# Channel sums of the norms moved from matmuls to adds, and the feed-forward's way back on four column groups

## The chip, the cores and the metric

The kernel runs on one core of a Trainium2 chip. The metric is the device time of one execution in microseconds, the median of several runs. The engines are named as in the profile: PE (TensorE, matmuls), PEld (its weight loads), DVE (VectorE), ACT (ScalarE), POOL (GpSimd) and SP (SyncE, which here only issues DMAs). Each engine runs its own instructions strictly in the order of the program.

## What is computed

Eight images x[384, 32, 32] go through two layers. Layer 0: an RMS norm over the 384 channels, a Mamba block (input projection, causal convolution, softplus deltas, a state scan with 16 states, gates, output projection) run in both directions over the 1024 positions, a depthwise 3x3 convolution with a sigmoid, and the residual. Layer 1: layer norm over the channels, causal attention with 6 heads of 64, residual; layer norm, a feed-forward of 384 to 1536 to 384 whose two weights are Kronecker products, residual.

```python
def rmsnorm(x, w, eps=1e-06):
    return x * jax.lax.rsqrt(jnp.mean(x * x, axis=-1, keepdims=True) + eps) * w

def step(h, inp):
    dA, dBu, c = inp
    h = dA * h + dBu
    return (h, jnp.einsum('bdn,bn->bd', h, c))

t = t + attn(_ln_t(t), ...)
w_fc, w_proj = jnp.kron(c_fc_1, c_fc_2), jnp.kron(c_proj_1, c_proj_2)
t = t + gelu(_ln_t(t) @ w_fc.T) @ w_proj.T
```

## The kernel before

**Layout.** Channels lie on the 128 partitions, so a tensor of one image is three channel tiles (c = 0, 1, 2) of 128 x 1024; positions are split in two halves of 512[...]. A batch is one image. Everything is float32 but the spread of the scan's input, which is bfloat16 in three parts.

**The stages of a batch b**, each a function: `project` (RMS norm, input projection), `gates`, `prepare` (causal convolution), `deltas` (softplus and what feeds the scan), `scans` (96 groups of 128 lanes each), `local` (3x3 convolution), `finish` (output projection, residual), `layernorm`, `attention`, `mix` (output projection, residual), `forward`. One scan group is: a DMA that broadcasts delta into a dA tile (one of 12 buffers), exp on ACT (L994), two small matmuls that spread the input (L1004, tile b), and for each half a multiply (L1009) and a scan (L1017) on DVE, then a product with C on POOL (L1020) and a sum by matmuls on PE (tile y, four column groups at a time). After each two block directions come uz on DVE (L970) and POOL (L975).

**Sums over channels.** They go across partitions and over three tiles, and are done on PE with a 128 x 128 matrix of ones, which leaves the sum on every partition. Each takes three matmuls that accumulate in one bank (`accumulate`, L422): in `project` over the squares (tile pss, L690), in `center` over the values (pm_a of the attention's norm, pm_f of the feed-forward's, L1068), in `deviation` over the squares of the centred values (pv_a, pv_f, L1091). `center` then subtracts on DVE (L1075), `deviation` squares on ACT (L1087, tiles lsq) and takes the reciprocal root on ACT (`rsqrt_mean`, L335 and L336), and `layernorm` multiplies on DVE (L1108).

**Feed-forward.** The Kronecker factor reduces the 384 inputs to 32 rows (tile y there named fy), PE makes 1536 hidden rows from them in pairs of banks (ph, `wide`), ACT applies gelu into a tile g that holds two of them (L1369), and `back` (L1373) accumulates them into bank pz, 32 output rows per matmul. A pair of hidden tiles goes to two of the four column groups of the array, and two such pairs make one round a; there are three rounds in each half.

**The order of the work** is not written out by hand. All stages record their operations in a `Plan` with an engine, a cost and a due time (`at`), and `Plan.run` (L170) places them greedily: of the operations ready on an engine the one due first is next. Four PSUM banks of kind psm, three of kind b, one y, 26 SBUF tiles of kind t and the 12 dA tiles are given out in that order as well. The due times come from windows (`PROJECT`, `NORM`, `FORWARD` and so on, L436 to L444), given in periods from the start of a batch's scans, from `PERIOD` and `HEAD` (L1401), and from offsets such as `EVICT`, `LOAD` and `PARTS`; `STAY` favours ACT operations that need no other function table, and `BACKLOG` limits how far SP issues DMAs ahead. The result is a fixed program: in the steady part of it, `project` and `gates` of batch b+2, `prepare` and `deltas` of b+1 (or so), and `finish` to `forward` of earlier batches stand among the scans of batch b.

Of the kernel before, what the change touches and what calls it, by code (L numbers as in the profile page):

```python
# [17 lines left out]
P = 128  # L18
B, C, H, W = 8, 384, 32, 32
L = H * W  # L20
CT = C // P
# [70 lines left out]
def pe(n, k=1):  # L92
    return k * (0.02 + n * 0.00185)
# [11 lines left out]
class Plan:  # L105
# [1 line left out]
    DRAIN = 0.19  # L107
    SLACK = 0.1
    SWITCH = 1.3
    STAY = 15.0  # L110
    BACKLOG = 10.0
    LANDING = 1.0
    DMA_LATENCY, DMA_RATE = 2.5, 262e3

# [173 lines left out]
def conv_attn_hybrid_kernel(  # L288
# [41 lines left out]
    def mm(out_, lhsT, rhs, first=True, last=True):  # L330
        return nc.tensor.matmul(out_, lhsT=lhsT, rhs=rhs, start=first, stop=last)  # L331
# [6 lines left out]
    def half(hf):  # L338
        return slice(hf * HALF, (hf + 1) * HALF)
# [93 lines left out]

    EVICT, MOVE, SUMS, PRODUCTS, DECAY, LOAD, PARTS = 27.83, 13.24, 12.22, -9.17, -222.27, -783.55, -339.2  # L436

    PROJECT, GATES, CONV, DELTA = (-1.525, -1.398), (-1.067, -0.985), (-0.952, -0.894), (-0.917, -0.358)
    LOCAL, OUTPUT, NORM, ATTEND = (0.593, 0.969), (1.016, 1.081), (1.16, 1.227), (1.191, 1.755)
    MIX, FORWARD = (1.81, 1.845), (1.879, 2.092)  # L440

    PROJECT0, EARLY, CONV0, DELTA0 = (-373.152, -337.008), (-788.581, -96.07), (-84.26, 78.46), (50.858, 257.144)
    GATES0, ZEROS, LATE, PROJECT1, GATES1 = (253.962, 443.889), (24.114, 455.177), (161.216, 306.444), (-92.709, 246.406), (452.944, 585.724)
    CONV1, DELTA1, LAYER1 = (164.85, 479.335), (392.72, 578.245), (462.639, 791.646)  # L444

    class Window:

# [216 lines left out]
    def project(b):  # L664

        xt = []
        for c in range(CT):
            t = tl(f"xt_{b}_{c}")
            dma(lambda t=t: t.t, lambda c=c: x[b, chans(c)].rearrange("p h w -> p (h w)"), [], [t], P * L * 4)
            xt.append(t)  # L670
        win = in_weights(b, 0)
        xp = [tl(f"xp_{b}_{c}", [P, PADDED]) for c in range(CT)]
        for c in range(CT):

            def border(c=c):
                xg = xp[c].t.rearrange("p (h w) -> p h w", w=WP)
                nc.gpsimd.memset(xg[:, 0 : H + 2 : H + 1, :], 0.0)
                nc.gpsimd.memset(xg[:, 1 : H + 1, 0 : W + 2 : W + 1], 0.0)

            op("POOL", 0.3, border, [], [(xp[c], "border")])  # L680
        sq = []
        for c in range(CT):
            t = tl(f"sq_{b}_{c}")
            op("ACT", act(L), lambda t=t, c=c: nc.scalar.activation(t.t, xt[c].t, AF.Square), [xt[c]], [t])
            sq.append(t)
        for hf in range(NH):
            p = bank(f"pss_{b}_{hf}")

            accumulate(
                [(lambda p=p, hf=hf, c=c: (p.t, ones, sq[c].t[:, half(hf)]), [sq[c]]) for c in range(CT)], p, pe(HALF), xp  # L690
            )
            op("ACT", 2 * act(HALF) + 0.1, lambda p=p: rsqrt_mean(p.t, eps6), [], [p], table=EXP)
            for c in range(CT):

                def scaled(p=p, hf=hf, c=c):
                    nc.vector.scalar_tensor_tensor(
                        inside(xp[c].t, hf), grid(xt[c].t[:, half(hf)]), col("norm_w", c), grid(p.t),
                        ALU.mult, ALU.mult,
                    )

                op("DVE", dve(HALF), scaled, [xt[c], p], [(xp[c], hf)])
        project.of[b] = xp
        into(b, 0, xp, win)
# [356 lines left out]

    def center(dst, src, n):

        for hf in range(NH):
            p = bank(f"pm_{n}_{hf}")

            accumulate(  # L1068
                [(lambda p=p, hf=hf, c=c: (p.t, ones, src[c].t[:, half(hf)]), [(src[c], hf)]) for c in range(CT)],
                p, pe(HALF), dst,  # L1070
            )
            for c in range(CT):
                op(
                    "DVE", dve(HALF),
                    lambda p=p, hf=hf, c=c: nc.vector.scalar_tensor_tensor(  # L1075
                        dst[c].t[:, half(hf)], p.t, -1.0 / C, src[c].t[:, half(hf)], ALU.mult, ALU.add
                    ), [p, (src[c], hf)], [(dst[c], hf)],
                )

    def deviation(dst, n, hf):  # L1080

        sqs = [tl(f"lsq_{n}_{hf}_{i}") for i in range(2)]
        p = bank(f"pv_{n}_{hf}")
        for c in range(CT):
            op(
                "ACT", act(HALF),
                lambda c=c: nc.scalar.activation(  # L1087
                    sqs[c // 2].t[:, half(c % 2)], dst[c].t[:, half(hf)], AF.Square
                ), [(dst[c], hf)], [(sqs[c // 2], c % 2)], holds=sqs,
            )  # L1090
        accumulate(  # L1091
            [
                (lambda c=c: (p.t, ones, sqs[c // 2].t[:, half(c % 2)]), [(sqs[c // 2], c % 2)])
                for c in range(CT)
            ], p, pe(HALF),
        )
        op("ACT", 2 * act(HALF) + 0.1, lambda: rsqrt_mean(p.t, eps5), [], [p], table=EXP)
        return p

# [228 lines left out]
    def forward(b, x2):  # L1328

        xn2 = [tl(f"xn2_{b}_{m}") for m in range(CT)]  # L1330
        center(xn2, x2, f"f{b}")
        y, z = tl(f"fy_{b}"), tl(f"fz_{b}")
        for hf in range(NH):
            p = bank(f"py_{b}_{hf}")

            accumulate(
                [
                    (
                        lambda p=p, hf=hf, c=c: (p.t, kr1[:, c].rearrange("p r i -> p (r i)"), xn2[c].t[:, half(hf)]),
                        [(xn2[c], hf)],  # L1340
                    )
                    for c in range(CT)
                ], p, pe(HALF), [y],
            )
            op("ACT", act(HALF), lambda p=p, hf=hf: nc.scalar.copy(y.t[:, half(hf)], p.t), [p], [(y, hf)])

            q = deviation(xn2, f"f{b}", hf)
            op(
                "DVE", dve(HALF), lambda q=q, hf=hf: nc.vector.tensor_mul(y.t[:, half(hf)], q.t, y.t[:, half(hf)]),
                [q], [(y, hf)],  # L1350
            )
        for hf in range(NH):
            pz = bank(f"pz_{b}_{hf}")
            for a in range(FT // RG):
                for r0 in range(0, RG, 2):

                    ph = [bank(f"ph_{b}_{hf}_{a}_{r0 + i}") for i in range(2)]

                    def wide(ph=ph, a=a, r0=r0, hf=hf):
                        for i in range(2):  # L1360
                            rows = slice((r0 + i) * KI, (r0 + i + 1) * KI)
                            mm(ph[i].t, w_fc1.t[rows, a, :], y.t[rows, half(hf)])

                    g = tl(f"g_{b}_{hf}_{a}_{r0}")
                    op("PE", pair(HALF), wide, [(y, hf), w_fc1], ph, holds=[g])

                    def gelu(ph=ph, g=g):
                        for i in range(2):
                            nc.scalar.activation(g.t[:, half(i)], ph[i].t, AF.Gelu)  # L1369

                    op("ACT", 2 * act(HALF), gelu, ph, [g], table=GELU)

                    def back(pz=pz, g=g, a=a, r0=r0):  # L1373
                        for i in range(2):
                            r = r0 + i
                            mm(
                                pz.t[r * KI : (r + 1) * KI, :], w_p1.t[:, a * RG + r, :], g.t[:, half(i)], a == 0,
                                a == FT // RG - 1,
                            )

                    op("PE", pair(HALF), back, [g, w_p1], [pz], holds=[z])
            op("ACT", act(HALF), lambda pz=pz, hf=hf: nc.scalar.copy(z.t[:, half(hf)], pz.t), [pz], [(z, hf)])
        ob = out[b].rearrange("(c p) h w -> c p (h w)", p=P)
        for m in range(CT):
            for hf in range(NH):
                p = bank(f"pe_{b}_{m}_{hf}")
                op(
                    "PE", pe(HALF), lambda p=p, m=m, hf=hf: mm(p.t, kr2.t[:, chans(m)], z.t[:, half(hf)]),
                    [(z, hf), kr2], [p],
                )  # L1390

                def add(p=p, m=m, hf=hf):
                    t = x2[m].t[:, half(hf)]
                    nc.vector.tensor_add(t, p.t, t)

                op("DVE", dve(HALF), add, [p], [(x2[m], hf)])
            dma(lambda m=m: ob[m], lambda m=m: x2[m].t, [x2[m]], [], P * L * 4)

    PERIOD, HEAD = 418.62, 167.66  # L1401

    def stretch(span, b):
        return Window(span[0] * PERIOD, span[1] * PERIOD, HEAD + b * PERIOD)
# [119 lines left out]
```

## Time and profile before

| what | value |
|---|---|
| median of 3 runs | 3935.32 us (3931.32 to 3963.04) |
| profiled execution: its time, its span | 3941.6 us, 3939.9 us |
| matmuls with ones (pss, pm_a, pm_f, pv_a, pv_f), records and busy time | 5 x 96 records, 51.1 + 47.4 + 45.9 + 46.1 + 47.8 us |
| feed-forward's way back (pz) | 384 records, 103.6 us |
| DMA | 858.92 MB, mean 218 GB/s |
| end of the scans of batch 0, 1, ... 7 | 555, 1003, 1449, 1905, 2353, 2806, 3267, 3686 us |
| mean granted clock of TensorE | 0.929 |

A float32 matmul appears as two records, so 96 records are 48 matmuls. Busy times of a group are unions: where two matmuls overlap, the time counts once. The line of most matmuls is L331, that of a helper, so they are told apart by their tiles. A row of a group gives its busy time, the mean ns of one, and after the second bar the idle time of its engine just before, with what ended it. Rows of the stretches give, for each engine, busy us and (in brackets) instructions, then the granted clock (1.00 is full), the share of the DMA engines and GB/s.

### The profile page before, as it was taken

To read this page: it belongs to the slowest core of one execution; us is meant where nothing else is said; L and a number is where in the kernel's file an instruction comes from. 1 tells how busy PE (TensorE), PEld (TensorE's weight loads), DVE (VectorE), ACT (ScalarE), POOL (GpSimd) and SP (SyncE) were. 2 spreads that over 40 slices of the span, in tenths; PEclk is the share of its full clock that TensorE was granted. 3 is DMA by queue.
4 is the path that set the end of the run, shared out by engine and by line. 5 is a ranking of instruction groups with operands and counts; after the bars stand their busy time and mean duration, and the time that the engine had idled before them with its cause. 6 is when DMAs were issued, how large, how long until landed. Compare 5 with 4: busy or idle time off the path is not lost.

```text
span 3939.9 us, 54075 instructions
## 1 busy us (share of the span) xinstructions
PE 3545.6 (90%) x17970; PEld 1386.8 (35%) x17970; DVE 3362.0 (85%) x4403; ACT 2821.3 (72%) x4465; POOL 2999.4 (76%) x2370
## 2 busy tenths in 40 slices
PE   7477768899999999899999999999999988999998
PEld 3011112443244432443234432443234431443363
DVE  1489998899988999899998999799898999999522
ACT  4665645887788867786788868887778866676464
POOL 2888986997699956998589966998579966676231
PEclk9587778999999999899999999999998998999999
DMA  8889899689966998689966998779976897678101
GB/s 266 238 253 281 250 262 245 179 235 269 273 201 201 259 264 244 183 241 256 276 207 187 255 271 249 199 230 248 257 231 170 219 253 189 168 197 227 44 9 37
DMA packets 301999, 858.92 MB, mean 218 GB/s; under 512 B 38312, under 2 KB 91576, under 8 KB 301720
## 3 DMA queue, kind: packets, MB, share of 16 engines
q1 hardware_dynamic: 301720, 855.47, 77.5%
q8 instruction: 143, 2.34, 0.3%
q14 instruction: 136, 1.11, 0.1%
HBM read 696.44 MB, written 160.68 MB: 218 GB/s over the span
## 4 chain that ended last, share of the span: by engine, by line
DVE 33%; PE 25%; DMA 15%; POOL 12%; issue 7%; ACT 7%; SPq 1%; POOLq 0%; DVEq 0%; ACTq 0%
DVE dA L1017 20%; DVE b L1009 7%; DMA dA<-ded 5%; POOL dA L1020 5%; PE t L1254 3%; PE pc L331 3%; PE y L331 2%; PE s L331 2%; PE pq L331 2%; POOL p L1244 2%; PE b L331 2%; DVE mx L1190 2%; DMA dusd<-part 1%; DMA yg<-ygd 1%; PE pi L331 1%
## 5 line engine op out<-in xcount | busy, mean ns | idle before, releaser
L1020 POOL TENSOR_TENSOR dA<-dA,bc 128x1024 f32<-128x1024 f32 x768 | 1808.7, 2366 | 579.5 <-DVE dA L1017 405.8
L1017 DVE TENSOR_TENSOR_SCAN dA<-dA,b 128x512 f32<-128x512 f32 x1536 | 1906.1, 1242 | 36.4 <-ACT dA L994 18.1
L1009 DVE TENSOR_TENSOR b<-b,bc 128x512 f32<-128x512 f32 x1536 | 986.3, 683 | 166.7 <-PE b L331 160.6
L994 ACT ACTIVATE dA<-dA,nA 128x1024 f32<-128x1024 f32 x768 | 864.3, 1146 | 311.6 <-DMA dA<-ded 270.6
L331 PE MATMUL b<-du,dup 32*128 32x512 bf16 x1536 | 412.9, 407 | 218.8 <-DVE dA L1017 160.4
L331 PE MATMUL y<-dA,sel 128*32 128x512 f32 x3072 | 485.3, 651 | 8.3 <-POOL dA L1020 6.3
L1190 DVE TENSOR_REDUCE mx<-s 128x1 f32<-128x512 f32 (+3 forms) x576 | 287.3, 546 | 170.2 <-PE s L331 166.3
L1197 ACT ACTIVATE p<-s,mx 128x512 f32<-128x512 f32 (+3 forms) x576 | 330.9, 580 | 115.6 <-DVE mx L1190 114.7
L1244 POOL TENSOR_SCALAR p<-p,den 128x512 f32<-128x512 f32 (+3 forms) x576 | 328.7, 590 | 83.4 <-DVE den L1236 66.8
L1254 PE MATMUL t<-ident,p 128*128 128x128 f32 x1728 | 286.2, 303 | 51.0 <-ACT p L1197 19.2
L331 PE MATMUL s<-k,q 64*128 64x512 f32 (+3 forms) x1152 | 302.7, 552 | 20.3 <-ACT p L1197 18.4
L1261 ACT COPY pT<-t 128x512 f32<-128x512 f32 (+1 forms) x480 | 245.5, 547 | 96.1 <-PE t L1254 87.9
L331 PE MATMUL pi<-xp,win 128*128 128x512 f32 x576 | 300.3, 640 | 13.9 <-ACT de L887 6.3
L1460 ACT ACT_TABLE_LOAD x224 | 287.4, 1283 | 4.7 <-PEq L1513 0.8
L331 PEld LDWEIGHTS <-dup 32*128 32x128 bf16 x1536 | 76.6, 92 | 593.9 <-issue 572.3
L1254 PEld LDWEIGHTS t<-ident,p 128*128 128x128 f32 x1728 | 208.3, 152 | 204.7 <-POOL p L1244 123.9
L331 PE MATMUL pc<-pT,v 128*64 128x128 f32 x3456 | 251.0, 291 | 6.2 <-ACT pT L1261 5.4
L331 PEld LDWEIGHTS pc<-pT,v 128*64 128x64 f32 x3456 | 199.6, 144 | 113.9 <-ACT pT L1261 52.9
L913 POOL TENSOR_TENSOR u<-u,part 128x1024 f32<-128x1024 f32 x96 | 205.2, 2138 | 26.0 <-ACT part L905 25.9
L905 ACT CAST part<-u 128x1024 bf16<-128x1024 f32 x144 | 150.5, 1045 | 88.5 <-DMA dusd<-part 45.2
L331 PEld LDWEIGHTS y<-dA,sel 128*32 128x32 f32 x3072 | 74.4, 111 | 296.1 <-POOL dA L1020 137.4
L331 PEld LDWEIGHTS s<-k,q 64*128 64x128 f32 x1152 | 110.5, 191 | 176.2 <-ACT p L1197 72.8
(183 smaller groups left out, 4741.8 us busy)
## 6 DMA issues: line engine op xcount, KB each, us to landing
dA<-ded SPq DMA_DIRECT2D x768, 512.0 KB
ct<-urd SPq DMA_DIRECT2D x96, 513.5 KB
du<-dusd SPq DMA_DIRECT2D x96, 512.0 KB
xs<-xpd SPq DMA_DIRECT2D x96, 432.8 KB
dusd<-part SPq DMA_DIRECT2D x288, 128.0 KB
ded<-de SPq DMA_DIRECT2D x48, 512.0 KB
uz<-uzd SPq DMA_DIRECT2D x48, 512.0 KB
bc<-bcd SPq DMA_DIRECT2D x32, 512.0 KB
```

What stands on the lines that cost most here:

```text
L331: return nc.tensor.matmul(out_, lhsT=lhsT, rhs=rhs, start=first, stop=last)
L913: "POOL", pool(L), lambda part=part: nc.gpsimd.tensor_sub(du.t, du.t, part.t), [part], [du]
L994: "ACT", act(L) + 0.1, lambda: nc.scalar.activation(dA.t, dA.t, AF.Exp, scale=nA.t[:, g : g + 1]),
L1009: "DVE", dve(HALF), lambda v=v, hf=hf: nc.vector.tensor_mul(v.t, v.t, bc.t[:, 0, half(hf)]), [(bc, 0)], [v],
L1017: nc.vector.tensor_tensor_scan(t, t, v.t[:, rev], h, ALU.mult, ALU.add)
L1020: op("POOL", pool(L), lambda: nc.gpsimd.tensor_mul(dA.t, dA.t, bc.t[:, 1]), [(bc, 1)], [dA], at=at - PRODUCTS)
L1190: lambda sc=sc, g=g, w=k1 - k0, hh=hh: nc.vector.tensor_reduce(mx.t[:, g, hh : hh + 1], sc[hh].t[:, 0:w], AX.X, ALU.max, negate=True), [sc ...
L1197: nc.scalar.activation(ps[g].t[:, hh, 0 : k1 - k0], sc[hh].t[:, 0 : k1 - k0], AF.Exp, bias=mx.t[:, g, hh : hh + 1], accum_out=den.t[:, g, ...
L1244: nc.gpsimd.tensor_scalar(t, t, den.t[:, g, hh : hh + 1], 1.0, ALU.mult, ALU.mult)
L1254: nc.tensor.transpose(t.t[:, o + j * P : o + (j + 1) * P], ps[g].t[:, hh, j * P : (j + 1) * P], ident)
L1261: nc.scalar.copy(pT[g].t[:, hs[0] : hs[-1] + 1, 0:w], t.t[:, 0 : len(hs) * w].rearrange("p (h w) -> p h w", w=w))
L1460: nc.scalar.preload_act_table_set(table)
```

## The change

Three things change.

- A new helper `summed` makes the sum over the three channel tiles with two adds of 128 x 512 and one matmul with ones. The adds are on POOL; with `last` they are on DVE. `center`, `deviation` and `project` call it. `project` keeps the three matmuls for batch 0; `last` is set in the norms of the last batch.
- `back` of the feed-forward waits for both gelu tiles of a round and issues the four matmuls of the round together, on four column groups.
- `STAY`, `BACKLOG`, `PERIOD`, `HEAD`, the offsets and all windows get other values, so the whole program is ordered anew.

```diff
-    STAY = 15.0
-    BACKLOG = 10.0
+    STAY = 10.0
+    BACKLOG = 20.0
...
-    EVICT, MOVE, SUMS, PRODUCTS, DECAY, LOAD, PARTS = 27.83, 13.24, 12.22, -9.17, -222.27, -783.55, -339.2
+    EVICT, MOVE, SUMS, PRODUCTS, DECAY, LOAD, PARTS = -6.07, 9.42, 15.82, 21.37, -209.94, -867.45, -103.51
-    LOCAL, OUTPUT, NORM, ATTEND = (0.593, 0.969), (1.016, 1.081), (1.16, 1.227), (1.191, 1.755)
-    MIX, FORWARD = (1.81, 1.845), (1.879, 2.092)
+    LOCAL, OUTPUT, NORM, ATTEND = (0.593, 0.928), (1.066, 1.131), (1.13, 1.14), (1.198, 1.736)
+    MIX, FORWARD = (1.775, 1.903), (1.774, 2.125)
...
-            accumulate(
-                [(lambda p=p, hf=hf, c=c: (p.t, ones, sq[c].t[:, half(hf)]), [sq[c]]) for c in range(CT)], p, pe(HALF), xp
-            )
+            if b == 0:
+                accumulate(
+                    [(lambda p=p, hf=hf, c=c: (p.t, ones, sq[c].t[:, half(hf)]), [sq[c]]) for c in range(CT)], p,
+                    pe(HALF), xp,
+                )
+            else:
+                summed(p, [(sq[c], half(hf), hf) for c in range(CT)], xp)
...
+    def summed(p, parts, holds, last=False):
+        engine, name, cost = (nc.vector, "DVE", dve(HALF) + 0.05) if last else (nc.gpsimd, "POOL", pool(HALF))
+        total = tl(f"sum_{p.name}", [P, HALF])
+        (t0, s0, k0), (t1, s1, k1), (t2, s2, k2) = parts
+        op(
+            name, cost, lambda: engine.tensor_add(total.t, t0.t[:, s0], t1.t[:, s1]), [(t0, k0), (t1, k1)], [total],
+            holds=list(holds),
+        )
+        op(name, cost, lambda: engine.tensor_add(total.t, total.t, t2.t[:, s2]), [(t2, k2)], [total])
+        op("PE", pe(HALF), lambda: mm(p.t, ones, total.t), [total], [p])
...
-            accumulate(
-                [(lambda p=p, hf=hf, c=c: (p.t, ones, src[c].t[:, half(hf)]), [(src[c], hf)]) for c in range(CT)],
-                p, pe(HALF), dst,
-            )
+            summed(p, [(src[c], half(hf), hf) for c in range(CT)], dst, n[1:] == str(B - 1))
...
+        summed(p, [(sqs[c // 2], half(c % 2), c % 2) for c in range(CT)], (), n[1:] == str(B - 1))
...
-                    def back(pz=pz, g=g, a=a, r0=r0):
-                        for i in range(2):
-                            r = r0 + i
-                            mm(
-                                pz.t[r * KI : (r + 1) * KI, :], w_p1.t[:, a * RG + r, :], g.t[:, half(i)], a == 0,
-                                a == FT // RG - 1,
-                            )
-
-                    op("PE", pair(HALF), back, [g, w_p1], [pz], holds=[z])
+                    gs.append(g)
+
+                def back(pz=pz, gs=gs, a=a):
+                    for r in range(RG):
+                        mm(
+                            pz.t[r * KI : (r + 1) * KI, :], w_p1.t[:, a * RG + r, :], gs[r // 2].t[:, half(r % 2)], a == 0,
+                            a == FT // RG - 1,
+                        )
+
+                op("PE", quad(HALF), back, gs + [w_p1], [pz], holds=[z])
...
-    PERIOD, HEAD = 418.62, 167.66
+    PERIOD, HEAD = 419.21, 278.5
```

## Prediction

> **What bounds the kernel now.** I read the page's shares first, then the busy time per batch, then the waits inside the steady stretch, because a share over the whole span mixes a head, seven equal periods and a tail.
>
> ```profile
> span 3939.9 us, 54075 instructions
> PE 3545.6 (90%) x17970; PEld 1386.8 (35%) x17970; DVE 3362.0 (85%) x4403; ACT 2821.3 (72%) x4465; POOL 2999.4 (76%) x2370
> ```
>
> PE and DVE are the two full engines; POOL has a quarter free. A batch's scans (L1017) end at 555, 1003, 1449, 1905, 2353, 2806, 3267 and 3686 us, so I cut the busy time there:
>
> ```profile
> core 0: us, PE busy (x) PEld busy (x) DVE busy (x) ACT busy (x) POOL busy (x), PEclk, DMA share, GB/s
> 123.00:555.00 432.00, 307.23 (x1044) 68.03 (x1043) 380.03 (x432) 264.74 (x284) 381.82 (x186) 0.74 0.91 260
> 1449.00:1905.00 456.00, 428.65 (x2246) 172.18 (x2245) 417.73 (x543) 354.32 (x561) 373.14 (x292) 0.96 0.85 234
> 1905.00:2353.00 448.00, 428.78 (x2246) 170.41 (x2245) 417.14 (x543) 353.88 (x562) 373.05 (x292) 0.96 0.82 238
> 3686.00:3940.00 254.00, 236.12 (x1290) 123.84 (x1288) 69.69 (x140) 127.11 (x323) 53.85 (x145) 0.98 0.09 33
> ```
>
> A period is 451 us (1003 to 2806 is four of them). In it PE works 428 (95%), DVE 417, POOL 373, ACT 354. So nothing can bring the period below 417 unless DVE's own work shrinks, and only 33 us of a period are open. The tail is PE's alone. What fills DVE's 33 idle us shows in its waits over three periods (window 1449 to 2806):
>
> ```profile
> engine line waited for: us in total, times, longest us
> DVE mx L1190 <- PE s L331: 35.7, 19, 7.6
> DVE xr L1108 <- ACT pv_a L336: 23.0, 6, 6.8
> DVE b L1009 <- PE b L331: 19.0, 18, 2.7
> ```
>
> PE being late (scores s, spreads b, and 2.8 for pg) costs DVE 57.5/3 = 19 us a period; the attention norm's chain through ScalarE costs 23.0/3 = 8. DVE almost never waits for POOL or through it: "dA from ACT" is 3.4 in the three periods.
>
> **The change, part by part.**
>
> *Matmuls with ones.* These are the prices:
>
> ```profile
> L331 PE MATMUL pm_a<-xr,ones 128*128 128x512 f32 x96 | 47.4, 616 | 0.0
> L331 PE MATMUL pss<-sq,ones 128*128 128x512 f32 x96 | 51.1, 654 | 4.0 <-ACT sq L684 4.0
> L975 POOL TENSOR_TENSOR uz<-uz 128x512 f32<-128x512 f32 x48 | 61.3, 1277 | 6.8 <-DVE uz L970 6.7
> L1394 DVE TENSOR_TENSOR x<-pe,x 128x512 f32<-128x512 f32 x48 | 32.3, 675 | 35.9 <-PE pe L331 35.9
> ```
>
> A matmul shows as two records, so 96 records are 48 matmuls: 47.4/48 = 0.99 us each (pss 1.06; the other three groups alike). Per period five sums (pss, pm and pv of attention, pm and pv of feed-forward) times two halves drop from three matmuls to one: 20 matmuls, -19.9 us of PE.
>
> *Way back of the feed-forward.* It had two column groups per step, now four. In the timeline four groups cost what two cost:
>
> ```profile
> 1003.96 1.05 PE L331 MATMUL pz<-g,w_p 128*32 128x512 f32 x4
> 1005.83 1.06 PE L331 MATMUL y<-dA,sel 128*32 128x512 f32 x8
> ```
>
> (4 records are 2 matmuls, 8 are 4). So 12 steps a batch become 6: 12 x 1.08 (103.6 us over 96 steps) less 6 x 1.2 (between this 1.06 and the 1.26 mean of y, 485.3/384) = -5.8. PE falls from 428 to 402.
>
> *What comes in.* 20 adds of 128x512 on POOL per period: 20 x 1.277 = +25.5, POOL 373 to 399. In the last batch the 16 adds stand on DVE (0.68 each), which idles there. In the built order 17 table loads come in on ACT (1.28 each, 2.7 a batch, into 97 idle us a period); all other counts, DMAs included, are unchanged: SP has the same 2000 entries in another order.
>
> *Rule against row.* The Trainium skill (GPSIMD Engine Reference, 4.1 Engine selection) says elementwise adds belong on VectorE, GpSimd being about 2x slower with two inputs. The rows agree on the price (1277 against 675) but not on the choice: by the rule the adds cost 20 x 0.675 = 13.5 a period on DVE, whose 417 is the floor, 7 x 13.5 = 95 us in all, which would leave about 3946; on POOL they fall into its 78 idle us. I cost them at nothing because DVE doesn't wait for POOL's products. If that cover goes: the four pss adds (5.1 us) stand in the built order at 55% of a scan, where POOL is 95 to 99% busy; the norm and feed-forward adds stand at 24 to 27% and 91 to 96%, where it is 56 to 78% busy. So 0 to +5 a period, and I take 0.
>
> *How much of PE's 26 us DVE gets.* Here a rule speaks against the change. Granted clock (column before DMA share) in two neighbouring stretches:
>
> ```profile
> 1500.00:1600.00 100.00, 96.11 (x432) 33.46 (x429) 91.57 (x118) 77.36 (x105) 78.16 (x40) 1.00 0.76 225
> 1600.00:1700.00 100.00, 90.73 (x553) 47.89 (x554) 83.23 (x113) 83.76 (x155) 94.66 (x88) 0.90 0.64 187
> ```
>
> PE 5.4 points less busy, clock 0.10 lower. The skill (TensorE: Matmul & The Clock Gate, Part 1) says idle windows drop the array to half clock. If PE goes from 95 to about 92%, the rows' slope gives 0.06 x 402 = 24 us of slower matmuls, the whole gain; if the new idle time is in short pieces, nothing is given back. I take half: 26 - 12 = 14 net. Of the 19 us of DVE's waits for PE I let 10 go; the rest is latency (a score matmul followed at once by its maximum).
>
> *The norm's wait.* POOL now stands twice in the chain subtract, squares, sum, rsqrt, multiply. In the built order of batches 1 to 5, between the third subtract of the first half and the first multiply (L1108), DVE has three subtracts, one b and two scans: 1.9 + 0.6 + 2.5 = 5.0 us of cover, where it had ten b, nine scans and a uz (about 20). But ACT's queue in between is shorter too: after the second square four logs (4.4), a square (0.6), three squares, a part and a dA (4.1), the rsqrt (1.2), 10.3 in all; POOL's adds (2.6) and the matmul (1.0) lie beside them. Wait 10.3 - 5.0 = 5.3, with 0.5 for the second half about 6, against 8 now: -2. Ends: 0 and 20 (POOL or a dA load late; everything of DVE queues behind L1108, and the q projections behind that).
>
> So g = 10 + 2 = 12 us a period, times seven periods: -84.
>
> *Places: the head.* The first b multiply is at 149.4, the first product on POOL at 157.4. Before that product POOL now has 33 ops of 128x1024 and 4 adds where it had 24: 9 x 2.36 + 4 x 1.28 = +26; ACT has 19 more entries before its first dA (+16). Against that batch 0's conv loads (ct) go ahead of batch 1's input, some 2 MB at 260 GB/s, -8. DVE may run ahead of POOL by 12 dA buffers, so POOL's +26 is covered, ACT's +16 isn't: +8 net, ends -10 and +25 (what was done early isn't in scan 0's way later: 380 of 432 there).
>
> *Tail.* In the chain pm_a, pm_f and pz of the last batch are on PE:
>
> ```profile
> 3698.26 5.16 PE pm_a L331 x12
> ...
> 3903.46 3.56 PE pz L331 x12
> ```
>
> Six matmuls (5.16) become two adds (1.36), one matmul (0.86) and the second half's 0.86 to 2.2: about -1.5 for each of pm_a and pm_f; pv's two, half of that; the way back loses 6 x 1.05 but waits for two gelus: -4. Sum -8.
>
> **Sum** against the profiled execution, 3941.6 us (span 3939.9 and 1.7 around it): +8 - 84 - 8 = 3857.6. The median, 3935.3, is 6.3 below that execution: 3851.
>
> **Rivals.** *(1) PE was the pace, all of its relief counts*: 25.7 x 7 = 180 and the tail: about 3750. For it: PE's 95%. Against: DVE's floor of 417 would leave 8 us idle a period. *(2) Nothing comes of it*: the freed PE time is given back by the clock and the waits for s are latency; only the tail and small gains: about 3925. For it: the stretches 900 to 1100, where feed-forward runs, have DVE at 99% already, and the relief falls mostly there. *(3) Slower: the norm's chain becomes DVE's stall.* Place: L1108, once a batch. POOL executes in order; its first pv add waits for ACT's squares with dA products behind it, and its second pv add stands behind uz and a product (3.6). If pv reaches ACT after the two dA there, and one of these waits for its load (longest 7.4), the wait grows from 8 to 28: +20 less PE's 10 is +10 a period, +70 with the tail and head neutral: about 4005. It decides when the wait at L1108 passes 18 us a batch. Against: POOL keeps 50 idle us. *(4) The parts do less than they say*: four groups with weights from two gelu tiles wait longer than a pair; worth under 6 x 7 = 42, inside the range.
>
> **How the numbers follow.** My forecast 0.53, (1) 0.14, (2) 0.18, (3) 0.15. The forecast's own range is 3777 to 3893 (g from 6 to 20, head's ends). A change of 1% (39 us) is about what a measurement can tell from none. Faster by over 1% (below 3896): the forecast and (1), 0.67; within: (2) and a little of (3), 0.20; slower: 0.13. The range leaves out 0.1 at each end: 3755 to 3975.
>
> **What would show it.** Right: PE between 3350 us busy (153 and 43 less) and 3430 (with the clock's share), POOL near 3180, DVE 3373; period 439; DVE's wait for PE s near 15 in three periods, L1108's near 6 a batch; granted clock near 0.91 (0.929 now). Wrong: L1108 over 18 a batch (3); PE still above 3450 with a lower clock, or DVE's waits for PE s as before (2); the first b multiply after 175 (head); periods of 425 (1).

## The result, and the profile after

| | before | after |
|---|---|---|
| median, measured together | 3938.73 us | 3962.07 us |
| profiled execution: span | 3939.9 us | 3952.6 us |
| end of the scans of batches 0 ... 7 | 555 ... 3686 | 562, 1005, 1458, 1915, 2366, 2824, 3281, 3706 |
| mean granted clock of TensorE | 0.929 | 0.906 |

The change makes the kernel slower by half a per cent: ratio 1.0047, 95% interval 1.0030 to 1.0064. The two profiled executions lie 12.7 us apart and the medians 23.3, so what is read from the traces below covers about half of the difference. The page of the changed kernel, its busy shares:

```profile
span 3952.6 us, 53660 instructions
PE 3430.8 (87%) x17658; PEld 1338.9 (34%) x17658; DVE 3374.8 (85%) x4419; ACT 2839.4 (72%) x4482; POOL 3167.4 (80%) x2510
```

PE lost 115 us of busy time and POOL gained 168, as worked out ahead. The same kernel cut at the ends of its own scans (head, two periods, tail), columns as in the prediction's table:

```profile
123.00:562.00 439.00, 290.97 (x1088) 69.16 (x1091) 370.65 (x421) 274.38 (x295) 387.11 (x190) 0.71 0.93 265
1458.00:1915.00 457.00, 416.18 (x2205) 165.53 (x2204) 418.13 (x542) 358.48 (x564) 397.07 (x312) 0.93 0.85 234
1915.00:2366.00 451.00, 411.97 (x2206) 163.00 (x2205) 418.06 (x544) 359.44 (x566) 397.26 (x312) 0.95 0.85 235
3706.00:3953.00 247.00, 223.96 (x1264) 118.42 (x1260) 81.59 (x158) 127.97 (x323) 53.81 (x145) 0.95 0.10 36
```

In a period PE works 12.5 and 16.8 us less, and still the period is 454.8 (1005 to 2824 is four) where it was 450.8 (1003 to 2806). The head is 7 longer, the tail 7 shorter, the seven periods 3144 against 3131: +13 in place of the -84. What DVE waits for in the changed kernel, window 1449 to 2806, in the columns of the prediction's waits:

```profile
DVE dA L1021 <- ACT dA L998: 44.7, 15, 5.4
DVE b L1013 <- PE b L331: 27.0, 30, 3.3
DVE mx L1199 <- PE s L331: 20.9, 26, 2.8
...
DVE xr L1117 <- ACT pv_a L336: 0.7, 2, 0.4
```

The norm's wait is gone (23.0 before), the wait for scores is 15 shorter, the one for b 8 longer, and a new one stands on top: the scan waits for its exponential, 44.7 where it was 3.4. All DVE waits of this window come to 104 us, before 97.

### The profile page after: what moved, and what is told of

The parts are those of the page before. It is cut to its first block, busy times and chain, and to the rows that moved or that the text cites. A ratio compares the mean times of both kernels' runs of the same rounds, so it can differ in the third digit from the quotient of the medians.

```text
span 3952.6 us, 53660 instructions
## 1 busy us (share of the span) xinstructions
PE 3430.8 (87%) x17658; PEld 1338.9 (34%) x17658; DVE 3374.8 (85%) x4419; ACT 2839.4 (72%) x4482; POOL 3167.4 (80%) x2510
## 4 chain that ended last, share of the span: by engine, by line
DVE 27%; PE 25%; POOL 21%; DMA 14%; issue 8%; ACT 4%; SPq 1%; POOLq 0%; DVEq 0%; ACTq 0%
DVE dA L1021 16%; POOL dA L1024 8%; DVE b L1013 6%; DMA dA<-ded 4%; PE pc L331 4%; PE y L331 3%; PE t L1263 3%; PE s L331 3%; POOL p L1253 3%; DVE mx L1199 2%; PE b L331 2%; PE pi L331 2%; DMA xs<-xpd 2%; POOL u L917 2%; DMA ct<-urd 2%
## 5 line engine op out<-in xcount | busy, mean ns | idle before, releaser
L331 PE MATMUL b<-du,dup 32*128 32x512 bf16 x1536 | 426.3, 415 | 250.7 <-DVE dA L1021 208.9
L331 PE MATMUL y<-dA,sel 128*32 128x512 f32 x3072 | 509.6, 670 | 49.3 <-POOL dA L1024 41.4
L331 PE MATMUL pi<-xp,win 128*128 128x512 f32 x576 | 286.9, 623 | 10.6 <-DMA win<-in_in_wT 4.6
L331 PE MATMUL pc<-pT,v 128*64 128x128 f32 x3456 | 260.1, 293 | 5.0 <-ACT pT L1270 4.3
```

## The experiments

In every experiment but three (a_early, code_only, places_only) the order of one of the two kernels is kept: after the planner has placed everything, an instruction does less, is left out, or gets another one in its place or beside it. Names beginning with b_ have the order of the kernel before, with a_ that of the changed one. "Before" is the kernel before, run on the same chip.

### The relief of TensorE alone: b_lean

```diff
 def term(...):                       # in accumulate, for pss of batches 1 to 7, pm and pv
-    mm(*args(), first, last)
+    if last: mm(*args())
 def back(...):
-    for i in range(2): r = r0 + i ... g.t[:, half(i)]
+    for r in range(RG) if r0 else (): ... g.t[:, half(r % 2)]
```

> The order of the kernel before, instruction for instruction, with TensorE's work cut as the change cuts it and nothing put in its place: of each norm's three matmuls with ones only the last is issued (two terms of the sum are left out, so the statistics are of one channel tile), and the way back of the feed-forward issues its four column groups with the second pair, which is read twice (the first pair is left out). No adds anywhere, no new places. Three theories. ORDER (the new places put four exponentials a period late on ScalarE; the relief itself is sound): 3840 to 3885 us, 50 to 100 under before, as my step g had it. LOAD (the relief is sound, but GpSimd's 20 adds a period take it back): the same 3840 to 3885, since no add is here. PACE (TensorE's work is not what paces the period, its relief is worth nothing and the clock takes it): 3915 to 3945.

Measured: 3953.06 us, 1.0027 (1.0010 to 1.0044) of before. Two of the three theories fall at once. With the order of before, no adds and 312 matmul records fewer, not a microsecond is gained; PACE comes nearest, though its range ended at 3945. One place shows why, the norm of batch 3. The kernel before, ACT, then DVE, then PE, from the timeline (start, duration, what; idle time before it in brackets):

```profile
1561.01 1.07 ACT L892 ACTIVATE e<-e 128x1024 f32<-128x1024 f32 x1
...
1564.38 1.15 ACT L895 ACTIVATE w<-w,minus 128x1024 f32<-128x1024 f32 x1
1565.44 0.64 ACT L335 ACTIVATE pv_a<-pv_a,eps 128x512 f32<-128x512 f32 x1
```

```profile
1566.73 1.89 DVE L1108 TENSOR_TENSOR xr<-pv_a,xr 128x512 f32<-128x512 f32 x3 [6.83 <-ACT pv_a L336]
```

```profile
1558.61 2.84 PE L331 MATMUL pv_a<-lsq_a,ones 128*128 128x512 f32 x6
1561.38 1.06 PE L331 MATMUL y<-dA,sel 128*32 128x512 f32 x8
1562.38 2.84 PE L331 MATMUL pv_a<-lsq_a,ones 128*128 128x512 f32 x6
1565.15 1.06 PE L331 MATMUL y<-dA,sel 128*32 128x512 f32 x8
1567.47 4.70 PE L331 MATMUL pq<-xr,wqkv 128*128 128x512 f32 x10 [1.26 <-DVE xr L1108]
```

And b_lean at the same place, ACT, then DVE, then PE:

```profile
1564.96 0.64 ACT L335 ACTIVATE pv_a<-pv_a,eps 128x512 f32<-128x512 f32 x1
```

```profile
1566.25 1.89 DVE L1114 TENSOR_TENSOR xr<-pv_a,xr 128x512 f32<-128x512 f32 x3 [6.83 <-ACT pv_a L336]
...
1574.86 0.70 DVE L1015 TENSOR_TENSOR b<-b,bc 128x512 f32<-128x512 f32 x1 [1.60 <-PE b L331]
```

```profile
1558.13 1.13 PE L331 MATMUL pv_a<-lsq_a,ones 128*128 128x512 f32 x2
1559.19 1.07 PE L331 MATMUL y<-dA,sel 128*32 128x512 f32 x8
1560.18 1.12 PE L331 MATMUL pv_a<-lsq_a,ones 128*128 128x512 f32 x2
1561.24 1.06 PE L331 MATMUL y<-dA,sel 128*32 128x512 f32 x8
1566.99 7.51 PE L331 MATMUL pq<-xr,wqkv 128*128 128x512 f32 x10 [4.69 <-DVE xr L1114]
```

The first sum is done at 1559.3 instead of 1561.5, but the root that follows it stands on ACT behind the four instructions of a softplus's logarithm (L892 to L895) and begins only at 1565.0, 0.5 earlier than before: DVE's wait is 6.83 in both. What PE saved became a gap of 4.69 us. And then the gap is paid for: the next ten records take 7.51 in place of 4.70, and DVE has a wait of 1.60 for b that wasn't there. The gap comes back in five batches, and each time the clock falls to half within 1 us of its end; such a wait for b follows in two of the five. The granted clock in these two stretches (column before the DMA share), before and b_lean:

```profile
1558.00:1567.00 9.00, 8.21 (x32) 2.43 (x28) 2.17 (x4) 8.30 (x11) 8.84 (x4) 1.00 1.03 254
1567.00:1575.00 8.00, 7.51 (x17) 2.88 (x18) 7.13 (x11) 7.78 (x10) 7.92 (x5) 1.00 1.03 247
```

```profile
1558.00:1567.00 9.00, 4.31 (x23) 0.92 (x21) 2.17 (x5) 8.16 (x11) 8.84 (x5) 0.95 0.94 253
1567.00:1575.00 8.00, 8.00 (x13) 3.23 (x14) 5.56 (x8) 6.44 (x8) 7.92 (x4) 0.63 1.03 286
```

1.00 became 0.63. The Trainium skill (TensorE: Matmul & The Clock Gate, Part 1) puts the drop to half clock after an idle window of about 3.4 us; gaps longer than that between matmuls are 6 in the whole trace of before, 10 in b_lean and 15 in the changed kernel. They fit the place above, but they are the smaller part. The traces' clock records are either full or half; the clock falls 62 times in before and 85 times in b_lean, and only 4 and 7 of these falls lie at such a gap. In the 3.4 us ahead of a fall PE was busy for 45% in the median, in both traces: gaps in small pieces lower the clock too. (No threshold comes out of this: the clock also stayed full after some pieces in which PE was busy for about half.)

In sum the time at half clock is 562 us in before and 754 in b_lean. These 192 us more are worth up to 96 us of matmuls (an estimate: half of them). Of the 196 us of work taken out (the prediction's 153 and 43), 76 show as less busy time (3546 to 3470). The clock explains most of the rest.

### By part, and the other way: b_lean_norm, b_lean_quad, b_heavy

b_lean_norm has only the first hunk of b_lean, b_lean_quad only the second. b_heavy adds to `term` for the same sums

```diff
     mm(*args(), first, last)
+    if norm and not last: mm(*args(), False, False)
```

> The norm part of b_lean alone: one matmul with ones for each sum instead of three (two terms left out), the way back as before. CLOCK: the clock falls to about 0.912 and the time stays, 3930 to 3960. If the time follows TensorE's work: 3860 to 3900.

> The feed-forward part of b_lean alone: the way back on four column groups with the second pair of tiles (the first pair is left out), the norms as before. CLOCK: the clock falls to about 0.922, 3935 to 3955. If the four-group matmuls themselves cost the clock: 0.91 or less and 3945 to 3965.

> The order of the kernel before with more work for TensorE: the first two of each norm's three matmuls with ones are issued twice (these terms count double in the sum), 40 more matmuls a period, about as many as the change takes out. CLOCK (TensorE's gaps set its clock, so that its work is elastic both ways): 3925 to 3955, with the granted clock at 0.935 or more. If TensorE's work is on the path when it grows: 3990 to 4060. BALANCE: 3990 to 4060 too. HAND-OFFS: 3940 to 3980.

| | b_heavy | before | b_lean_quad | b_lean_norm | b_lean |
|---|---|---|---|---|---|
| ratio to before | 1.0170 (1.0119 to 1.0220) | 1 | 1.0010 (0.9985 to 1.0035) | 1.0005 (0.9985 to 1.0025) | 1.0027 |
| granted clock | 0.933 | 0.929 | 0.923 | 0.910 | 0.905 |
| PE busy, us | 3648 | 3546 | 3532 | 3475 | 3470 |

Medians 4014.21, 3947.59 and 3944.70 us (b_heavy, quad, norm). The norms' matmuls taken out lower the clock; the feed-forward's hardly do (executions of b_lean_quad gave 0.918 to 0.925, those of before beside them 0.920 to 0.931). Neither piece gains anything. But PE's work isn't elastic both ways: with 20 matmuls more a period (40 records; the 40 matmuls of the expectation are a slip) the clock rises by only 0.004 and the time by 1.7%, above what CLOCK and HAND-OFFS gave and in the range of BALANCE. So CLOCK alone is too simple: added work is on a path, removed work isn't.

### The adds: b_lean_load and a_narrow

b_lean_load is b_lean with, in place of the left-out matmuls, `nc.gpsimd.tensor_add(extra, src, ...)` of 128x512. a_narrow changes `summed`:

```diff
-    engine.tensor_add(total.t, t0.t[:, s0], t1.t[:, s1])   (and the second add)
+    the same on [:, 0:16]
-    mm(p.t, ones, total.t)
+    mm(p.t, ones, flat, True, False); mm(p.t[:, 0:16], ones, total.t[:, 0:16], False, True)
```

> As b_lean, and GpSimd does two adds of 128x512 for each norm sum at the places of the two left-out matmuls, into a scratch tile that nobody reads: the change's load on GpSimd without its wait and without its order. ORDER: within 15 us of b_lean. LOAD: at least half of b_lean's gain goes again, products come 4 us later and tiles of dA come free later, 3890 to 3950. PACE: as before, 3915 to 3950.

> The changed kernel in its own order, with GpSimd's adds of the norms narrowed from 512 to 16 columns (the rest of the sum is left out: the matmul takes a constant tile and adds the 16 columns to it), so that waits and order stay and some 24 us a period of GpSimd's work go. The DVE adds of the last batch stay. LOAD: 3870 to 3910 us, 45 to 90 under the changed kernel, and VectorE's wait for dA falls from 14 to under 6 us a period. ORDER: 3935 to 3960, the wait for dA stays at 11 or more, since ScalarE's order holds the exponentials back. PACE: 3940 to 3965.

Measured: b_lean_load 4006.62 us, 1.0161 (1.0137 to 1.0185), which is 54 us over b_lean and over what any theory gave. In the order of before the adds are far from free. DVE's waits of the window 1449 to 2806 show where they come in (b_lean, then b_lean_load):

```profile
DVE xr L1114 <- ACT pv_a L336: 22.9, 6, 6.8
DVE fac L1234 <- POOL fac L1231: 0.5, 2, 0.4
```

```profile
DVE xr L1118 <- ACT pv_a L336: 35.9, 6, 6.8
DVE fac L1238 <- POOL fac L1235: 10.6, 4, 3.3
```

These two waits grow by 23.1 us in three periods, 7.7 a period, which over seven periods is about the 54 us. Both come through POOL's order. In the attention's softmax the small operations for `fac` stand behind three adds of pss (at 1757 to 1765). In the norm the second half's root stands on ACT behind a copy (`part`), which waits for a product u on POOL, and that product now has four adds of pv_a between the products ahead of it. The copy in b_lean; then b_lean_load, ACT, POOL and DVE:

```profile
1566.68 1.04 ACT L911 CAST part<-u 128x1024 bf16<-128x1024 f32 x1 [0.47 <-POOL u L908]
```

```profile
1615.25 1.04 ACT L915 CAST part<-u 128x1024 bf16<-128x1024 f32 x1 [4.80 <-POOL u L912]
1616.20 0.65 ACT L335 ACTIVATE pv_a<-pv_a,eps 128x512 f32<-128x512 f32 x1
```

```profile
1610.52 1.05 POOL L438 TENSOR_TENSOR extra<-lsq_a 128x512 f32<-128x512 f32 x1
1611.65 1.26 POOL L438 TENSOR_TENSOR extra<-lsq_a,extra 128x512 f32<-128x512 f32 x1
1612.87 2.35 POOL L912 TENSOR_TENSOR u<-de,u 128x1024 f32<-128x1024 f32 x1
```

```profile
1617.50 1.89 DVE L1118 TENSOR_TENSOR xr<-pv_a,xr 128x512 f32<-128x512 f32 x3 [5.13 <-ACT pv_a L336]
```

The last wait is 0.8 in b_lean. PE too waits longer for POOL's products (the sums y: 29.8 us over the run in place of 10.3), but DVE's waits for b, s and pg hardly grow (67.0 to 69.5 in three periods), so this is not where the time goes.

a_narrow takes the adds' work away again in the changed order and measures 3954.45 us, 1.0037 (1.0019 to 1.0056), with the changed kernel at 1.0047: no gain that can be told from noise. It isn't a clean test, for each sum gets a second, narrow matmul and PE is 35 us busier (3466 against 3431); at b_heavy's rate (67 us slower for 102 us more) that could hide some 20 us. Still the two waits of the old order are nearly gone in the changed kernel (0.7 and 3.4 in three periods): the adds' cost of LOAD is real in the old order, and in the new one none is seen.

### The new wait for exponentials: a_early

After `Plan.run` has sorted the program, an exponential of dA for which DVE stands still in the plan is moved ahead on ACT to where its load is due (23 of 768; the 384 in the expectation is a slip):

```diff
+    while k and acts[k - 1][0] >= o.ready and acts[k - 1][2].table in (None, o.table): k -= 1
+    if k < i: moved[id(o)] = acts[k][0] - 1e-3
+order = sorted((moved.get(id(o), st), n, o) for st, n, o in order)
```

> The changed kernel, complete, with only those exponentials of dA moved ahead on ScalarE (23 of 384, about four a period, past 1 to 16 instructions each, up to the time at which the plan has their load landed) for which VectorE stands still in the plan. ORDER: 3865 to 3915 us, and VectorE's wait for dA falls from 14 to under 5 us a period. LOAD: the exponential then waits for its load, which comes late because the tile came free late: 3940 to 3965, the wait for dA stays over 10. PACE: the wait goes but another takes its place: 3940 to 3965.

Measured: 3949.92 us, 1.0029 (1.0014 to 1.0043). That is the whole computation, some 0.2% under the changed kernel, which the intervals don't tell from none, and not under before. In its waits, same window:

```profile
DVE b L1030 <- PE b L348: 38.2, 28, 5.4
DVE mx L1216 <- PE s L348: 35.2, 23, 4.7
DVE dA L1038 <- ACT dA L1015: 13.5, 9, 2.4
DVE xr L1134 <- ACT pv_a L353: 6.9, 6, 2.2
```

The exponentials do come (44.7 to 13.5, so their loads were there in time), and the 31 us are waited out elsewhere: b +11, scores +14, norm +6. ORDER and LOAD fall, PACE is right again: take one wait out and another takes its place.

### The two halves of the change: code_only, places_only

code_only is the changed kernel with the constants of before (`STAY` to `LAYER1`, `PERIOD`, `HEAD`), places_only the kernel before with the changed one's.

> The changed code (adds on GpSimd, way back on four column groups) with the planner's constants and places of the kernel before: half of the change alone. If the places only retune what the code gives: 3900 to 3970. If the order is what decides, and the constants belong to one code: 3980 to 4080.

> The code of the kernel before with the constants and places of the changed one: the other half alone. If the new places are good in themselves: 3900 to 3970. If they belong to the new code: 3980 to 4080.

Measured: 4038.99 us, 1.0257 (1.0216 to 1.0299), and 4015.02 us, 1.0195 (1.0156 to 1.0233). The constants belong to their code. Without new places the changed code costs 2.6%; they win back 2.1 of that.

### Which engine sets the period: b_dve, b_pool, b_act, b_dma and sums of them

```diff
-    nc.vector.tensor_mul(v.t, v.t, bc.t[:, 0, half(hf)])                     b_dve: [:, 0:384]
-    nc.gpsimd.tensor_mul(dA.t, dA.t, bc.t[:, 1])                             b_pool: [:, 0:912]
-    nc.scalar.activation(dA.t, dA.t, AF.Exp, ...)                            b_act: [:, 0:704]
-    dma(ct[g]) for g in 0..3                                                 b_dma: for g in 0..2, conv reads ct[min(g, 2)]
-    mm(y.t[rows, :], sel, hs[r].t[:, half(hf)])                              b_y: the first 256 columns, uz too
```

b_lean_dve is b_lean and b_dve, a_dve is b_dve's edit in the changed kernel, b_all is b_lean with the first four, b_all_y has b_y's edit besides.

> The kernel before in its own order, with one engine relieved by some 26 us a period, here VectorE: the multiply of b with the input projection covers 384 of 512 columns (the rest is left unmultiplied), 192 a period by 0.136 us. b_lean has shown that the same relief of TensorE brings nothing in this order; the question is now which engine's relief does. VECTOR (the period is VectorE's own work and waits that do not shrink): 3720 to 3800 us, most of 26 x 8. GPSIMD (GpSimd, 98% busy for 270 us of each period, paces that part and hands its lag on through the tiles of dA): 3860 to 3900, only the part of the period in which GpSimd has room gets shorter. BALANCE (all engines pace in turn, none alone is worth anything): 3900 to 3940.

> As b_dve, with GpSimd relieved by some 25 us a period: its product of dA with the output projection covers 912 of 1024 columns (the rest is left unmultiplied), 96 a period by 0.26 us. VECTOR: 3915 to 3945. GPSIMD: 3800 to 3870, since 60% of the 25 us lie in the stretch in which it is full, times 7 to 8. BALANCE: 3900 to 3940.

> As b_dve, with ScalarE relieved by some 25 us a period: the exponential of dA covers 704 of 1024 columns (the rest stays as loaded), 96 a period by 0.27 us. VECTOR: 3900 to 3940 (ScalarE is on the waits for the norm and for the scores, so a little may come). GPSIMD and BALANCE: 3910 to 3945.

> As b_dve, with the DMA engines relieved by some 22 us a period: the shifted load of the causal convolution is left out for the fourth of each four tiles (the matmul reads the third's instead), 3 of 12 loads of 0.51 MB a period out of 27 MB. If the DMA engines, full for nearly half of the period, pace it: 3780 to 3850. VECTOR, GPSIMD and BALANCE: 3925 to 3945.

> The order of the kernel before with both reliefs at once: TensorE's of b_lean (two terms of each norm's sum and the first pair of the way back left out) and VectorE's of b_dve (b multiplied over 384 of 512 columns). Alone they brought +0.3% and -1.0%. PAIR (TensorE and VectorE pace each other: what one is relieved of it spends waiting for the other): more than the sum, 3780 to 3860 us. SUM (what holds is elsewhere, in latencies through ScalarE and GpSimd or in the fixed order): the sum of the two, 3890 to 3925.

> The changed kernel in its own order with b_dve's relief of VectorE (b multiplied over 384 of 512 columns). In the kernel before this was worth 41 us. PAIR: TensorE has been relieved here, so it is worth twice as much or more, 3830 to 3880. SUM: again 30 to 50, 3905 to 3930.

> The order of the kernel before with all five reliefs at once: TensorE's of b_lean, VectorE's of b_dve, GpSimd's of b_pool, ScalarE's of b_act and the loads of b_dma (each leaves out what was said there), 22 to 26 us a period on every engine. BALANCE (the engines are near their limits together, whichever is relieved the next one holds): 3730 to 3800 us, most of 25 us in each of 8 periods. HAND-OFFS (the period is made of waits from one engine to the next in a fixed order, which no engine's own work enters much): 3850 to 3900, not far under b_dve.

> The order of the kernel before with TensorE relieved evenly along the whole period, by some 20 to 25 us: the sums over the states take 256 of 512 columns (the rest is left out), 48 instructions of four column groups a period at half their width. PLACE (TensorE paces the middle of the period, and the change's relief lay elsewhere): 3790 to 3860, and the stretches of attention get 2 us shorter for each 8 groups. HAND-OFFS: 3920 to 3950, with the granted clock lower again, 0.915 or less.

> All reliefs of b_all and the narrower sums of b_y: now each engine has 22 us or more a period less to do, in every stretch of the period. PLACE or BALANCE: 3720 to 3790, at least 100 under b_all. HAND-OFFS: 3850 to 3890, b_all or a little under it.

| relieved | median, us | ratio to before, interval |
|---|---|---|
| b_dve | 3896.01 | 0.9900 (0.9867 to 0.9934) |
| b_pool | 3939.68 | 1.0008 (0.9985 to 1.0030) |
| b_act | 3964.55 | 1.0066 (1.0040 to 1.0092) |
| b_dma | 3931.31 | 0.9984 (0.9966 to 1.0003) |
| b_y (PE, evenly) | 3914.39 | 0.9927 (0.9907 to 0.9946) |
| b_lean_dve | 3906.20 | 0.9914 (0.9886 to 0.9942) |
| a_dve | 3926.14 | 0.9945 (0.9923 to 0.9967) |
| b_all | 3891.01 | 0.9846 (0.9785 to 0.9907) |
| b_all_y | 3853.23 | 0.9792 (0.9763 to 0.9822) |

By their traces DVE, POOL, ACT and PE's sums y were each relieved of 22 to 24 us a period. The DMA engines were not: b_dma leaves out 1.5% of their bytes (858.92 to 846.30 MB), about 5 us a period of their busy time; the 22 us and the 27 MB of the expectation are slips. So none of the four computing engines alone is worth more than 1% of the 5% or so that it was relieved of. VECTOR and GPSIMD are out; BALANCE in its pure form too, since b_all brings 52 us and not 150 or more. What the DMA engines would give stays open. PAIR is out: PE's relief adds nothing to DVE's (0.9914 against 0.9900), and DVE's is worth no more in the changed kernel, where PE is relieved, than in the one before (1.0% of before in each: 1.0047 to 0.9945, and 1 to 0.9900). b_y lies between its two theories: evenly laid, PE's relief is worth 25 us, where the change's places made it worth nothing. A few of the 25 may be DVE's, whose uz is narrowed too (3362 to 3347 us busy). b_all_y is the sharpest; its page:

```profile
span 3841.9 us, 54426 instructions
PE 3306.6 (86%) x17658; PEld 1372.9 (36%) x17658; DVE 3158.7 (82%) x4403; ACT 2619.4 (68%) x4465; POOL 2811.7 (73%) x2370
```

Each computing engine has 188 to 239 us less to do than before, and the span is 98 shorter: DVE's idle time rose from 578 (3939.9 - 3362.0) to 683. Its clock is 0.887. Cutting each trace at every eighth scan group, mean of batches 2 to 6, gives the twelve stretches of a period in us (first row absolute, the others as the difference to it):

| stretch | 1 | 2 | 3 | 4 | 5 | 6 | 7 | 8 | 9 | 10 | 11 | 12 | sum |
|---|---|---|---|---|---|---|---|---|---|---|---|---|---|
| before | 31.6 | 34.8 | 36.1 | 40.4 | 35.8 | 51.1 | 32.3 | 38.4 | 39.3 | 39.2 | 38.3 | 35.5 | 453.0 |
| b_lean | 0.0 | +0.6 | +0.1 | +1.9 | -1.5 | +0.4 | 0.0 | -0.3 | +0.5 | +0.1 | +0.1 | +0.1 | +2.0 |
| b_pool | +0.8 | +1.1 | 0.0 | -0.2 | -0.3 | -0.2 | -0.2 | -0.3 | -0.8 | 0.0 | +0.3 | -0.1 | -0.2 |
| b_all_y | -3.4 | -0.4 | -1.7 | +0.7 | -1.8 | -0.7 | -1.8 | -2.0 | -1.1 | 0.0 | -0.6 | +0.6 | -12.4 |
| after | -0.6 | -2.5 | -2.4 | +3.2 | -2.9 | -12.8 | +6.4 | +3.3 | +3.4 | +5.8 | +1.6 | 0.0 | +2.5 |

In an order that is kept, even relief of all four computing engines moves no stretch but the first by more than 2 us. Most of what is moved in the last row is the new order: the 6th stretch has fewer scores to make (34 records where before had 58) and the 7th more (30, had 6).

One rival is left. In stretches 1, 2 and 10 to 12 the DMA engines are full (a share of 1.00 to 1.03, mean of the same batches in before), and no run relieved them in the last three. These take 113 us in before and in b_all_y, with less work on every computing engine. The three in batch 3, before and b_all_y:

```profile
1781.20:1897.10 115.90, 108.35 (x594) 38.94 (x594) 110.00 (x143) 80.77 (x124) 84.96 (x72) 0.99 1.02 255
```

```profile
1748.10:1859.30 111.20, 99.77 (x578) 38.30 (x570) 103.86 (x144) 72.85 (x124) 77.83 (x72) 0.92 1.03 267
```

One batch alone says little (in batch 4 they take 110.6 and 119.1). Against this rival stands the first stretch, where DMA is as full and b_all_y is 3.4 shorter; nor can it explain stretches 3 to 9, where DMA is at 0.60 to 0.85 and which shorten by only 8.4 in all. It is not tested.

## Why the prediction was wrong

**Right.** Head: +8 said, +7 measured (555 to 562). Tail: -8 said, -7 measured. Of the head's parts only the start was read again: the first b multiply came 13 us later (149.4 to 162.4), and 6 of them were made up. PE's busy time came to the forecast's upper end (3430), POOL's, DVE's and the clock's (0.906 for 0.91) as said. The net relief, "26 - 12 = 14", was 12.5 and 16.8 in the two periods above: the clock did give about half back, though the half had been assumed and not worked out. The norm's wait went, even further than "-2": 23.0 to 0.7 in three periods is -7.4 each.

**The step that failed is g = 10 + 2**, a sum that takes waits of DVE away one by one and leaves all others as they were. The period became 4 us longer, not 12 shorter. In g it is first "of the 19 us of DVE's waits for PE I let 10 go". These were waits for an instruction on PE, not for PE's work. Without adds, in the same order, b_lean has 32.9 + 27.8 + 6.3 = 67.0 us of them in three periods against 57.5: longer by 3 a period. One place is shown in the fences of b_lean: the removed matmuls lay where the result had to wait for ScalarE's queue, the time saved became a gap of PE, and the gap cost clock in the projections after it. In that window it accounts for 1.6 of the 9.5 us; that the lower clock made the rest is likely, with 192 us more at half clock, but not shown. In the changed kernel the same three waits came to 47.9, 3 a period less, not 10. With the norm's 7.4 the two terms came to 10.6 of the 12 after all, by luck: neither was right by itself.

**Second, the adds "at nothing because DVE doesn't wait for POOL's products".** It doesn't, but it waits for other work of POOL that queues behind the adds: `fac`, and through ScalarE the norm's root. In the old order this costs 54 us over the run, about 7 a period, above the upper end of 5. In the new order no such cost is seen. Whether DVE would have been the better place for the adds was not tried.

**Third, a wait that the sum didn't hold.** The new order makes the scans wait for their exponentials, +13.8 a period. It isn't a separate loss either, since removing it (a_early) brought the kernel some 0.2%, within noise. The three periods add up: -7.4 norm, -4.9 scores, -2 reciprocals, +13.8 exponentials, +2.7 b and small ones: from 97 to 104 us, +2.5 a period, which is what the stretches give. (The stated range has a slip as well: a g of 6 with the head's +25 ends at 3910, not at 3893.)

Rival (2), "nothing comes of it", was the right kind with 3925; it missed by 37, and it priced neither the adds nor the order. With the runs the account is, against before: relief +0.3% (b_lean), the adds' load in the old order +1.3% (b_lean_load less b_lean), and a new order that wins back 1.1% of these 1.6%. PE with its 95% is not the pace, and neither is DVE, ScalarE or GpSimd alone. **Open:** which hand-offs make up the period is not settled, only that relieving these four evenly leaves about half of the relief as waiting (DVE: 203 us less work, 105 more idle); whether the DMA engines hold the stretches in which they are full; nor why the shorter exponentials of b_act made the kernel 0.7% slower; nor what takes the time in stretches 7 to 10 of the changed kernel beyond the work moved there. No version that beats both kernels with the whole computation came out of this.

## What to carry to other kernels

A wait named after an engine is not a wait for that engine's work: follow the late instruction on its own engine, and count the relief only where it shortens the last link. When work is put on an engine that has room, look at everything that queues behind it there, not only at its main product. When work is taken from TensorE, look at the gap that it leaves and at the granted clock of the matmuls after it. And where a planner fixes the order, measure an edit in the old order first, with nothing else changed; if it brings nothing there, a new order has to bring everything.

## What the runs showed that was not expected

- Granted clock follows the work taken from PE: 0.929, then 0.910 without the norms' matmuls, 0.905 with a shorter feed-forward besides and, with 239 us less busy time, 0.887. Most falls to half clock come without a gap of 3.4 us (78 of 85 in b_lean).
- Added and removed work aren't symmetric: 20 matmuls a period more cost 1.7%, as many fewer bring nothing; 20 adds a period more on GpSimd cost 1.3%, and 23 us a period fewer of its work bring nothing (b_pool).
- ScalarE relieved of 190 us over the run left the kernel 0.7% slower.
